# Moving the attention keys next to their batch, fixing the places of the first feed-forward, and moving one product behind the last transposes

## The chip, the core and the metric

The kernel runs on one core of a Trainium2 chip. Its engines work side by side and each takes its own instructions in order: PE (TensorE, matrix products and transposes, with a weight load PEld ahead of each), DVE (VectorE), ACT (ScalarE), POOL (GpSimd) and SP, which here only issues transfers. The metric is the device time of one execution in microseconds (us).

## The reference

Four batches of 512 tokens with 512 features pass through four residual steps. `ctx` holds 512 tokens of 128 features for each batch.

```python
x = x + tanh(g_xattn[0]) * L0_xattn(ctx, layernorm(x))   # learned adjacency
x = x + tanh(g_ffn[0])   * L0_ffn(layernorm(x))          # Hadamard, 8-bit, ternary weights
x = x + tanh(g_xattn[1]) * L1_xattn(layernorm(x), ctx)   # 16 heads, latent keys
x = x + tanh(g_ffn[1])   * L1_ffn(layernorm(x))          # rms norm, 8-bit, ternary weights

# L0_xattn: sim = Q K^T of ctx; in each row the 153 largest are kept (threshold), sigmoid,
#           A = (A + A^T) / 2, and a mix with the normalised x
# L0_ffn:   h = fwht(x) quantised to 8 bits; u = silu(h Wg) * (h Wu); fwht(u) quantised; u Wd
# L1_xattn: q_big = rope(x Wq w_kc_q), kv_r = rope(ctx)
#           q_r = q_big W_qr, k_r = kv_r W_kr          (64 numbers for each of the 16 heads)
#           attn = softmax(q_r k_r^T); ctx_c = attn kv_r; out = ctx_c w_kc_kv Wo
# L1_ffn:   value * silu(gate) of quantised x, quantised, w_out
```

The keys `k_r` depend on `ctx` alone, and those of a batch are first needed when that batch's attention begins.

## The kernel before

The kernel has three stages: a prologue for batch 0, the attention of all four batches with the other work woven between its steps, and a tail with the last feed-forward of batch 3. The flag `alone[0]` is true in the prologue and in the tail.

**Prologue.** Three generators are stepped by turns: `adjacency(0)` (the top-k of batch 0, 20 rounds of `max` and `match_replace` for each tile of 128 rows, lines 436 and 441), `feed_weights` (ternary weights for the first feed-forward) and `ahead()`. `ahead()` rotates `ctx` into `kv` for all batches on POOL, multiplies the two output matrices of each of the 16 heads into one (`pO`, line 668, copied by ACT and stored to DRAM as `omd`), transposes the four `kv` (`pkv`, line 678), and then makes the keys: for each of 8 pairs of heads one weight `wk` is loaded (line 685), and for each of the four batches one product `pk` of 128x512 (line 688), one ACT copy to `krs` (line 690), and one store by POOL's queue to the DRAM tile `krd` (line 692). Attention loads `kr` back from `krd` (line 783). The feed-forward of batch 0, `feed0(0)`, follows; `ahead()` is stepped once for each of its steps.

**The first feed-forward.** Each of four tiles is normalised, turned and quantised; its gates (`pg`, `pu`, line 291) are multiplied into `ya` (line 297); `back` runs four butterfly stages of two halves each between `ya` and `yb` on DVE (line 538), four transposes and small Hadamard products on PE (`ph`, line 544, and `pzh`, line 550) with ACT copies between, the largest value `amaxh` (line 364; in four parts at line 359 for the last tile), the quantisation to `q` (lines 369 and 197), transposes of `q` (`ptq_h`, line 191) and the down product `pd` (line 386). `big()` gives `ya` and `yb` their place: while `alone`, three of five calls take the ring `big` of three buffers, and two take the ring `pT` of two, by a counter that the weight loads use too. A ring's next tile waits for the readers of the tile that had its buffer.

**Attention.** It walks through 32 pairs of heads, 8 for each batch. In each of four steps `j` of a pair it computes scores (`pss`, lines 806 and 809), their largest value (`nm`, line 814, DVE), the exponentials (line 817, ACT) and the division (line 820); it transposes the probabilities two steps later (`turn`, `ppt`, line 828, copied to `pT` at line 829). Between these stand the queries of the next pair: `head` (`pqh`, line 747) and `rope` (`pb`, line 762, then `ro` and `rs` on DVE, lines 770 to 775, and their sum on POOL, line 776). At the end of a pair `rotated()` loads `kr` and multiplies the rotated queries into `q_r` (`pr`, lines 733 and 735; ACT copy `qr`, line 793), the last two `turn` follow, then `attended` (`pc`, line 836) and `added` (`po`, line 848, with the sum on DVE at line 853).

**What is woven in.** `jobs` holds for each batch `b` from 1 to 3 a generator `before(b)`: `adjacency(b)`, then `feed0(b)`; it must be finished when the attention of batch `b-1` ends. The last job makes the ternary weights of the second feed-forward and runs `feed1` of batches 0 to 2. After each step of a pair the loop takes as many steps of the job as its costs allow.

**What sets the order.** The source order is a priority only: a scheduler places each instruction on its engine. `tc.high_priority(offset=-FILL)` with `FILL = 800` gives the top-k a lower priority, so that it fills DVE between the attention's own instructions. PSUM has the pools `mm` (4 banks), `tr` (2) and `bg` (2). `bg_tr` gives every fourth transpose a `bg` bank while `alone`, otherwise every one. `front_t` alternates between the rings `front` (3 buffers) and `pp` while `alone`, otherwise it takes `front`.

Of the kernel before, what the change touches and what calls it, by code (L numbers as in the profile page):

```python
# [9 lines left out]
F32 = mybir.dt.float32  # L10
BF = mybir.dt.bfloat16
# [4 lines left out]
P = 128  # L16
B, S, D = 4, 512, 512
NT = S // P
NC = D // P
FF = 2048  # L20
# [13 lines left out]
def flamingo_kernel(  # L34
# [9 lines left out]
    nc = tc.nc  # L44
# [4 lines left out]
    dram = ctx.enter_context(tc.tile_pool(name="dram", bufs=1, space=bass.MemoryType.DRAM))  # L49

    bp = ctx.enter_context(tc.tile_pool(name="bg", bufs=1))
    hp = ctx.enter_context(tc.tile_pool(name="heads", bufs=2))
    wp = ctx.enter_context(tc.tile_pool(name="attn", bufs=2))
# [4 lines left out]
    def mm_ps(name):  # L58
        return ps.tile([P, 512], F32, tag="mm", name=name)

    def tr_ps(name):
        return pst.tile([P, 4, P], F32, tag="tr", name=name)


    alone = [True]
# [9 lines left out]
    def gate_ps(name):  # L75
        return mm_ps(name) if alone[0] else bg_ps(name)

    def bg_tr(name, dt=F32):
        if mine("tr", 4):
            return psb.tile([P, 4, P], dt, tag="bg", name=name)  # L80
        return pst.tile([P, 4, P], dt, tag="tr", name=name)

    def two_k(tag, bufs, name):
        return bp.tile([P, 512], F32, tag=tag, name=name, bufs=bufs)

    def front_t(name):
        if mine("front", 2):
            return two_k("front", 3, name)
        return wp.tile([P, 512], F32, tag="pp", name=name, bufs=7)
# [6 lines left out]
    def back_t(name):  # L96
        return two_k("back", 2, name)

    def big(name):
        turn_of["big"] += 1  # L100
        if not alone[0] or turn_of["big"] % 5 in (1, 3, 0):
            return bp.tile([P, FF], F32, tag="big", name=name, bufs=3)
        t = wp.tile([P, NT, S], F32, tag="pT", name=name)
        return t.rearrange("p j s -> p (j s)")

    ident = const.tile([P, P], F32, tag="ident", name="ident")
# [32 lines left out]
    def drain(gen):  # L139
        try:  # L140
            while True:
                next(gen)
        except StopIteration as e:
            return e.value
# [157 lines left out]
    def tiles(name, ready, wa, back, spread):  # L302

        def gate(j):
            zq, dg, du = ready[j]
            y = big(f"ya_{name}_{j}")
            return gated(f"{name}_{j}", zq, wa, dg, y), back(j, y, du)  # L310

        def go(gen, parts):
            for _ in range(parts):
                next(gen, None)

        if not alone[0]:
            last = iter(())
            for j in range(NT):
                if j == 2:
                    reached.append(name)  # L320
                front, behind = gate(j)
                yield from woven(front, last)
                last = behind
            yield from last
            return
        front, cur = gate(0)
        drain(front)
        last = None
        for j in range(NT):
            front, after = gate(j + 1) if j + 1 < NT else (iter(()), None)  # L330
            for k in range(8 if spread else 4):
                if spread:
                    go(cur, 1)
                if k % 2 == 0 or not spread:
                    go(front, 1)
                yield 0.0
            if spread:
                if last:
                    go(last, 4)
                go(cur, 4)  # L340
            else:
                go(cur, 4)
            if last:
                drain(last)
            last, cur = cur, after
        drain(last)
        yield 0.0
# [47 lines left out]
    FILL = 800  # L395
# [240 lines left out]
    NG = NH // 2  # L636
# [4 lines left out]
    def ahead():  # L641

        cos_k = wp.tile([P, NT, DC], F32, tag="rs", name="cos_k", bufs=3)
        nc.gpsimd.dma_start(cos_k, cosk)
        sin_k = wp.tile([P, NT, DC], F32, tag="rs", name="sin_k", bufs=3)
        nc.gpsimd.dma_start(sin_k, sink)
        kvT = []
        hf = DC // 2  # L650
        for b in range(B):
            cb = wp.tile([P, NT, DC], F32, tag="qh", name=f"cb_{b}")
            nc.gpsimd.dma_start(cb, cx[b * S : (b + 1) * S, :].rearrange("(j p) d -> p j d", p=P))
            t = const.tile([P, NT, DC], F32, tag=f"kv{b}", name=f"kv_{b}")
            nc.gpsimd.tensor_tensor(t, cb, cos_k, ALU.mult)
            rt = wp.tile([P, NT, DC], F32, tag="rs", name=f"rt_{b}", bufs=3)
            nc.gpsimd.tensor_tensor(rt[:, :, :hf], cb[:, :, hf:], sin_k[:, :, :hf], ALU.mult)
            nc.gpsimd.tensor_tensor(rt[:, :, hf:], cb[:, :, :hf], sin_k[:, :, hf:], ALU.mult)
            nc.gpsimd.tensor_tensor(t, t, rt, ALU.add)
            kv[b] = t  # L660
        yield
        for h in range(NH):
            wv = hp.tile([P, DC], F32, tag="wk", name=f"wv_{h}", bufs=3)
            nc.sync.dma_start(wv, wkckv[h])
            wo = wp.tile([P, D], F32, tag="rs", name=f"wo_{h}", bufs=3)
            nc.sync.dma_start(wo, woT[h])
            po = mm_ps(f"pO_{h}")
            nc.tensor.matmul(po, wv, wo, start=True, stop=True)
            om = wp.tile([P, D], F32, tag="cxo", name=f"oms_{h}", bufs=3)
            nc.scalar.copy(om, po)  # L670
            d = dram.tile([P, D], F32, tag=f"om{h}", name=f"omd_{h}")
            nc.gpsimd.dma_start(d, om)
            om_d[h] = d
            yield
        for b in range(B):
            pt = tr_ps(f"pkv_{b}")
            for j in range(NT):
                nc.tensor.transpose(pt[:, j, :], kv[b][:, j, :], ident)
            tT = two_k("gate", 2, f"kvT_{b}") if b < 2 else hp.tile([P, S], F32, tag="om", name=f"kvT_{b}")
            nc.scalar.copy(tT, pt.rearrange("p j q -> p (j q)"))  # L680
            kvT.append(tT)
            yield
        for g in range(NG):
            wk = hp.tile([P, P], F32, tag="wk", name=f"wk_{g}", bufs=3)
            nc.sync.dma_start(wk, wkr[g])
            for b in range(B):
                pk = mm_ps(f"pk_{b}_{g}")
                nc.tensor.matmul(pk, wk, kvT[b], start=True, stop=True)
                k = wp.tile([P, S], F32, tag="cxo", name=f"krs_{b}_{g}", bufs=3)
                nc.scalar.copy(k, pk)  # L690
                d = dram.tile([P, S], F32, tag=f"kr{b}_{g}", name=f"krd_{b}_{g}")
                nc.gpsimd.dma_start(d, k)
                kr_d[b, g] = d
                yield

    def hidden_T(b):
        mv, r = ln_stats([xs[b, j] for j in range(NT)], f"q{b}")
# [162 lines left out]
    def attention(first):  # L860


        order = [(b, g) for b in range(B) for g in range(NG)]
        cur = first
        for at, (b, g) in enumerate(order):
            nxt = begin(*order[at + 1]) if at + 1 < len(order) else None
            cur.oms = out_weights(b, g)
            fresh = nxt is not None and nxt.b != b
            for j in range(NT):
                cur.scores(j)  # L870
                if nxt:
                    if j == 0:
                        if fresh:
                            hidden_T(nxt.b)
                        nxt.head(0)
                    elif j == 1:
                        nxt.rope(0)
                        nxt.head(1)
                    elif j == 2:
                        nxt.rope(1)  # L880
                    else:
                        nxt.rope(2)
                if j > 1:
                    cur.turn(j - 2)
                yield b, g
            if nxt:
                nxt.rotated()
            cur.turn(NT - 2)
            cur.turn(NT - 1)
            cur.attended()  # L890
            cur.added()
            if g == NG - 1 and b < B - 1:
                for j in range(NT):
                    d = dram.tile([P, D], F32, tag=f"xd{b}_{j}", name=f"xd_{b}_{j}")
                    nc.sync.dma_start(d, xs[b, j])
                    spilled[b, j] = d
            cur = nxt
# [5 lines left out]
    def step(gen, parts):  # L903
        for _ in range(parts):
            next(gen, None)
# [38 lines left out]
    w1 = []  # L944

    def before(b):
        yield from adjacency(b)
        yield from feed0(b, w0)

    def last_weights():  # L950
# [164 lines left out]
```

## Time and profile before

| | us |
|---|---|
| median of 3 runs | 2082.72 (2080.54 to 2085.15) |
| the profiled execution | 2086.76 |
| its span, first to last instruction | 2085.0 |
| first scores of the attention (copy of the first `qr`) | 290.0 |
| `qr` copies of the first pairs of batches 1, 2, 3 | 701.9, 1123.1, 1544.4 |
| `qr` copy of the last pair | 1923.4 |

The profile lists busy times of the engines; a row of a group ends with the idle time before it and with what ended it. A matmul with 32-bit operands stands in the records as two halves. In timelines the first two numbers are start and duration, and square brackets give the idle time of the engine before the instruction and what it waited for.

### The profile page before, as it was taken

Reading aid. Unit: us, or ns where it says so; the run is one execution under the profiler, and the core shown is the slowest. Engines: PE = TensorE matmul, PEld = TensorE weight load, DVE = VectorE, ACT = ScalarE, POOL = GpSimd, SP = SyncE. Lnnn points to the kernel's source line nnn. Section 1 sums busy time; section 2 is a strip of 40 time slices with the busy share of each in tenths; the row PEclk is TensorE's granted clock in tenths of the full one; section 3 lists DMA queues with packets and bytes.
Section 4 is the critical chain, followed back from the end, with each engine's and each line's share of the span. In section 5 each row is a group of like instructions: output and inputs, shape, how many; then the busy total and the mean of one; then the engine's idle time right before and its main releaser. Section 6 shows DMA issues by size and latency. Waiting matters only on the chain.

```text
span 2085.0 us, 21677 instructions
## 1 busy us (share of the span) xinstructions
PE 1864.1 (89%) x7274; PEld 876.8 (42%) x7274; DVE 1589.9 (76%) x3233; ACT 1182.9 (57%) x1982; POOL 331.0 (16%) x316
## 2 busy tenths in 40 slices
PE   1269889999999999999989999999889999999898
PEld 0135433444544444444544444445443444444444
DVE  6997689996675999967668999676645745856775
ACT  6936634354744554455455553554799565567554
POOL 3011121122101121131011211310111200111000
PEclk9779989999999999999999999999999999999999
DMA  7442211110100211111002111110656111111000
GB/s 268 149 141 107 83 37 48 44 46 27 38 20 27 86 50 41 47 32 33 25 27 87 49 47 38 37 33 20 224 185 225 55 31 46 57 32 46 11 16 26
DMA packets 62175, 137.66 MB, mean 66 GB/s; under 512 B 7152, under 2 KB 14704, under 8 KB 58992
## 3 DMA queue, kind: packets, MB, share of 16 engines
q1 hardware_dynamic: 56592, 120.35, 18.2%
q0 software_dynamic: 4320, 14.16, 1.8%
q10 hardware_dynamic: 1152, 1.77, 0.2%
q8 instruction: 58, 0.95, 0.2%
q14 instruction: 53, 0.43, 0.1%
HBM read 116.33 MB, written 19.92 MB: 65 GB/s over the span
## 4 chain that ended last, share of the span: by engine, by line
PE 52%; DVE 29%; ACT 11%; DMA 3%; POOL 2%; issue 2%; ACTq 0%; SPq 0%; POOLq 0%; DVEq 0%
PE pc L836 8%; PE po L848 6%; PE pqh L747 6%; DVE work L441 4%; DVE m L436 4%; DVE nm L814 4%; PE pb L762 3%; PE pzh_f L550 3%; PE pr L733 3%; PE pss L806 3%; PE pu_f L291 2%; DVE rs L775 2%; PE pg_f L291 2%; DVE ro L770 2%; PE pu_g L291 2%; PE pd_g L386 2%
## 5 line engine op out<-in xcount | busy, mean ns | idle before, releaser
L776 POOL TENSOR_TENSOR ro<-ro,rs 128x512 f32<-128x512 f32 x192 | 250.3, 1306 | 1333.8 <-DVE rs L772 722.5
L817 ACT ACTIVATE pp<-pss,nm 128x512 f32<-128x512 f32 x256 | 175.1, 688 | 224.6 <-DVE nm L814 223.9
L747 PE MATMUL pqh<-hT,wq 128*128 128x512 f32 x512 | 240.6, 609 | 4.0 <-ACT pp L817 2.5
L836 PE MATMUL pc<-pT,kv 128*128 128x512 f32 x512 | 233.5, 598 | 6.0 <-ACT pT L829 6.0
L848 PE MATMUL po<-om,cxo 128*128 128x512 f32 x512 | 231.4, 596 | 0.5 <-ACT cxo L841 0.5
L814 DVE TENSOR_REDUCE nm<-pss 128x1 f32<-128x512 f32 x256 | 167.6, 680 | 70.4 <-PE pss L809 70.0
L762 PE MATMUL pb<-qh,wc 128*128 128x512 f32 x384 | 191.7, 617 | 7.4 <-DVE ro L770 3.8
L436 DVE MAX8 m<-work 128x8 f32<-128x512 f32 x304 | 197.6, 680 | 0.5
L441 DVE MATCH_REPLACE8 work<-m,work 128x512 f32<-128x512 f32 x288 | 192.9, 675 | 0.1
L820 ACT ACTIVATE pp<-pp,rsm 128x512 f32<-128x512 f32 x256 | 179.2, 725 | 17.7 <-DVE rsm L819 17.1
L829 ACT COPY pT<-ppt 128x512 f32<-128x512 f32 x256 | 143.2, 590 | 36.9 <-PE ppt L828 36.8
L828 PE MATMUL ppt<-ident,pp 128*128 128x128 f32 x1024 | 149.3, 280 | 11.4 <-ACT pT L829 9.2
L853 DVE SCALAR_TENSOR_TENSOR x<-po,gt,x 128x512 f32<-128x512 f32 x128 | 94.5, 743 | 82.6 <-PE po L848 81.5
L828 PEld LDWEIGHTS ppt<-ident,pp 128*128 128x128 f32 x1024 | 116.4, 142 | 92.5 <-issue 45.6
L806 PE MATMUL pss<-kr,qr 64*128 64x512 f32 x256 | 145.6, 649 | 9.0 <-ACT pp L817 7.5
L747 PEld LDWEIGHTS pqh<-hT,wq 128*128 128x128 f32 x512 | 93.7, 193 | 126.9 <-issue 93.1
L809 PE MATMUL pss<-kr,qr 64*128 64x512 f32 x256 | 145.5, 649 | 0.0
L848 PEld LDWEIGHTS po<-om,cxo 128*128 128x128 f32 x512 | 94.4, 190 | 113.7 <-issue 95.7
L770 DVE TENSOR_TENSOR ro<-pb,cos_q 128x512 f32<-128x512 f32 x192 | 130.4, 679 | 15.1 <-PE pb L762 14.3
L836 PEld LDWEIGHTS pc<-pT,kv 128*128 128x128 f32 x512 | 93.0, 191 | 102.8 <-issue 90.5
L733 PE MATMUL pr<-ro,wr 128*64 128x512 f32 x192 | 100.6, 625 | 29.5 <-POOL ro L776 28.3
L841 ACT COPY cxo<-pc 128x512 f32<-128x512 f32 x64 | 37.5, 586 | 135.3 <-PE pc L836 135.1
(266 smaller groups left out, 3132.8 us busy)
## 6 DMA issues: line engine op xcount, KB each, us to landing
wq<-in_wqh SPq DMA_DIRECT2D x64, 256.0 KB, 2.7
om<-omd SPq DMA_DIRECT2D x64, 256.0 KB, 2.7
wc<-in_wkcq SPq DMA_DIRECT2D x32, 384.0 KB, 3.1
krd<-krs POOLq DMA_DIRECT2D x32, 256.0 KB, 2.5
kr<-krd SPq DMA_DIRECT2D x32, 256.0 KB, 2.7
sa_w1v<-in_gvT SPq DMA_DIRECT2D x8, 1024.0 KB, 5.6
sb_w1v<-in_gvT SPq DMA_DIRECT2D x8, 1024.0 KB, 5.5
wr<-in_wqr SPq DMA_DIRECT2D x32, 192.0 KB, 2.4
```

The lines of the kernel that those rows point to most:

```text
L436: nc.vector.max(m8[j], cur[j])
L441: nc.vector.match_replace(works[j], m8[j], cur[j], GONE)
L747: nc.tensor.matmul(pq, self.wqs[i][:, c, :], hT[self.b][:, c, :], start=(c == 0), stop=(c == NC - 1),)
L762: nc.tensor.matmul(pb, self.wc[:, at : at + P], self.qhs[i if i < 2 else o], start=True, stop=True)
L776: nc.gpsimd.tensor_tensor(ro, ro, rs, ALU.add)
L806: nc.tensor.matmul(*args, start=True, stop=True)
L814: nc.vector.tensor_reduce(nm, pss[i], AX.X, ALU.max, negate=True)
L817: nc.scalar.activation(pp, pss[i], AF.Exp, bias=nm, accum_out=sm)
L820: nc.scalar.activation(pp, pp, AF.Copy, scale=rs)
L828: nc.tensor.transpose(pt[:, l, :], pp[:, l * P : (l + 1) * P], ident)
L836: nc.tensor.matmul(pc, kv[self.b][:, l, :], self.pT[i][:, l, :], start=(l == 0), stop=(l == NT - 1),)
L848: nc.tensor.matmul(po, self.cxo[i][:, j * P : (j + 1) * P], self.oms[i], start=(i == 0), stop=(i == 1),)
```

## The change

1. Of the keys, `ahead()` makes only those of batch 0. A new generator `keys(b)` makes those of one batch: it transposes `kv[b]`, copies it to a tile in the ring `q`, and for each pair of heads loads `wk`, multiplies, copies and stores. `before(b)` steps it once for every sixth step of `adjacency(b)`, at a priority lower by 200. Each batch loads the 8 weights anew: 32 loads where there were 8.
2. In the feed-forward of batch 0 the eight calls of `big()` take their places from a list: `b` is the ring `big`, `t` the ring `pT`, and `h` the buffer `hT`, which the adjacency of batch 0 had and which the transposed input of the attention takes next. In the order of the calls they are ya 0, ya 1, yb 0, ya 2, yb 1, ya 3, yb 2, yb 3.
3. `nxt.rotated()` stands behind the last two `turn`.

```diff
+    lent = []
+
     def big(name):
+        place = lent.pop(0) if lent else None
+        if place == "h":
+            t = hp.tile([P, NC, S], F32, tag="hT", name=name, bufs=1)
+            return t.rearrange("p c s -> p (c s)")
+        if place == "t":
+            t = wp.tile([P, NT, S], F32, tag="pT", name=name)
+            return t.rearrange("p j s -> p (j s)")
+        if place == "b":
+            return bp.tile([P, FF], F32, tag="big", name=name, bufs=3)
         turn_of["big"] += 1
...
+        if spread:
+            lent.extend("btbhtbbt")
         front, cur = gate(0)
         drain(front)
...
-        for b in range(B):
-            pt = tr_ps(f"pkv_{b}")
-            for j in range(NT):
-                nc.tensor.transpose(pt[:, j, :], kv[b][:, j, :], ident)
-            tT = two_k("gate", 2, f"kvT_{b}") if b < 2 else hp.tile([P, S], F32, tag="om", name=f"kvT_{b}")
-            nc.scalar.copy(tT, pt.rearrange("p j q -> p (j q)"))
-            kvT.append(tT)
+        yield from keys(0)
+
+    def keys(b):
+
+        pt = bg_tr(f"pkv_{b}")
+        for j in range(NT):
+            nc.tensor.transpose(pt[:, j, :], kv[b][:, j, :], ident)
+
+        kvT = bp.tile([P, FF], BF, tag="q", name=f"kvT_{b}").bitcast(F32)[:, 0:S]
+        nc.scalar.copy(kvT, pt.rearrange("p j q -> p (j q)"))
+        yield
+        for g in range(NG):
+            wk = hp.tile([P, P], F32, tag="wk", name=f"wk_{b}_{g}", bufs=3)
+            nc.sync.dma_start(wk, wkr[g])
+            pk = gate_ps(f"pk_{b}_{g}")
+            nc.tensor.matmul(pk, wk, kvT, start=True, stop=True)
+            if alone[0]:
+                k = wp.tile([P, S], F32, tag="cxo", name=f"krs_{b}_{g}", bufs=3)
+            else:
+                k = front_t(f"krs_{b}_{g}")
+            nc.scalar.copy(k, pk)
+            d = dram.tile([P, S], F32, tag=f"kr{b}_{g}", name=f"krd_{b}_{g}")
+            nc.gpsimd.dma_start(d, k)
+            kr_d[b, g] = d
             yield
-        for g in range(NG):
-            wk = hp.tile([P, P], F32, tag="wk", name=f"wk_{g}", bufs=3)
-            nc.sync.dma_start(wk, wkr[g])
-            for b in range(B):
-                pk = mm_ps(f"pk_{b}_{g}")
-                nc.tensor.matmul(pk, wk, kvT[b], start=True, stop=True)
-                k = wp.tile([P, S], F32, tag="cxo", name=f"krs_{b}_{g}", bufs=3)
-                nc.scalar.copy(k, pk)
-                d = dram.tile([P, S], F32, tag=f"kr{b}_{g}", name=f"krd_{b}_{g}")
-                nc.gpsimd.dma_start(d, k)
-                kr_d[b, g] = d
-                yield
...
+            cur.turn(NT - 2)
+            cur.turn(NT - 1)
             if nxt:
                 nxt.rotated()
-            cur.turn(NT - 2)
-            cur.turn(NT - 1)
...
     def before(b):
-        yield from adjacency(b)
+        k = keys(b)
+        for n, cost in enumerate(adjacency(b)):
+            yield cost
+            if n % 6 == 5:
+
+                with tc.high_priority(offset=-FILL // 4):
+                    step(k, 1)
+        drain(k)
         yield from feed0(b, w0)
```

## The prediction

> **What bounds the kernel now.** I read the page first, then busy time by windows, the pk tile, the DVE timeline of the prologue, and the PE waits of the attention.
>
> The page says that PE is the busiest engine, and that its bad slices are the first six (the prologue, before the first scores at 290 us) and the tail:
>
> ```profile
> PE 1864.1 (89%) x7274; PEld 876.8 (42%) x7274; DVE 1589.9 (76%) x3233; ACT 1182.9 (57%) x1982; POOL 331.0 (16%) x316
> ...
> PE   1269889999999999999989999999889999999898
> ...
> DVE  6997689996675999967668999676645745856775
> ...
> PEclk9779989999999999999999999999999999999999
> ```
>
> By windows (us; then PE, PEld, DVE, ACT, POOL busy, granted clock, DMA share, GB/s) the feed-forward of batch 0 has a middle where PE never rests, and edges where it does:
>
> ```profile
> 125.00:150.00 25.00, 13.75 (x69) 8.80 (x68) 19.98 (x61) 8.87 (x16) 1.62 (x3) 0.73 0.16 56
> 150.00:175.00 25.00, 24.84 (x116) 13.10 (x115) 24.86 (x51) 15.37 (x25) 4.31 (x8) 1.00 0.31 111
> 175.00:200.00 25.00, 24.95 (x147) 15.54 (x145) 14.78 (x18) 19.40 (x33) 5.34 (x9) 1.00 0.27 101
> 200.00:225.00 25.00, 24.82 (x119) 13.48 (x119) 24.84 (x32) 15.87 (x28) 6.59 (x12) 1.00 0.33 124
> 225.00:250.00 25.00, 19.43 (x128) 12.45 (x126) 14.53 (x29) 14.00 (x24) 1.62 (x3) 1.00 0.18 58
> ```
>
> The key products lie in exactly this middle:
>
> ```profile
> L688 PE MATMUL pk<-kvT,wk x64: 592/592/648, 156.7 to 231.9; 128*128 128x512 f32 x64
> L690 ACT COPY krs<-pk x32: 566/586/657, 158.1 to 232.5; 128x512 f32<-128x512 f32 x32
> ```
>
> The 64 records are 32 products; a group of four records fills 1.72 us of the chain, so one costs PE 0.86 us, 27.5 us for all. The DVE timeline shows who is late for it: the gate of tile 3 waits 6.44 us for PE, then the butterfly of tile 2 2.33 us:
>
> ```profile
> 183.17 2.28 DVE L364 TENSOR_REDUCE amaxh_f<-yb_f 128x1 f32<-128x2048 f32 x1
> ...
> 196.47 0.69 DVE L297 TENSOR_TENSOR ya_f<-sg_f,pu_f 128x512 f32<-128x512 f32 x1 [6.44 <-PE pu_f L291]
> 199.49 2.36 DVE L538 TENSOR_TENSOR yb_f<-ya_f 128x1024 f32<-128x1024 f32 x2 [2.33 <-PE ph_f L544]
> ...
> 228.85 2.29 DVE L364 TENSOR_REDUCE amaxh_f<-yb_f 128x1 f32<-128x2048 f32 x1 [1.12 <-ACT yb_f L551]
> ```
>
> In the attention, the first four pairs of a batch carry the top-k of the next batch's adjacency. There both PE and DVE are nearly full, DVE more so; the last four carry the feed-forward and are PE's:
>
> ```profile
> 701.90:742.80 40.90, 38.92 (x121) 16.49 (x122) 40.51 (x95) 20.82 (x40) 7.62 (x6) 1.00 0.31 98
> 742.80:782.90 40.10, 38.51 (x118) 16.30 (x119) 39.91 (x92) 17.54 (x37) 7.64 (x6) 1.00 0.16 48
> 782.90:824.10 41.20, 38.64 (x125) 16.80 (x125) 39.27 (x86) 22.36 (x43) 7.61 (x6) 1.00 0.17 47
> 824.10:864.80 40.70, 38.52 (x122) 16.39 (x122) 40.22 (x92) 17.78 (x37) 7.62 (x6) 1.00 0.17 47
> 864.80:1123.10 258.30, 245.97 (x1035) 122.71 (x1036) 184.20 (x328) 133.38 (x245) 43.53 (x40) 0.98 0.11 32
> ```
>
> What PE waits for from 290 us on (total, times, longest): above all the last rotated chunk of the next pair, added on POOL, in front of q_r's product:
>
> ```profile
> PE pr L733 <- POOL ro L776: 24.1, 23, 1.6
> PE ppt L828 <- ACT pT L829: 9.2, 29, 1.6
> ...
> PE pc L836 <- ACT pT L829: 6.0, 16, 1.9
> ```
>
> **Part 1, keys moved: the prologue.** By the built order, 13 products stay ahead of the first scores (8 of batch 0, 5 of batch 1), so PE loses 19 x 0.86 = 16.3 us there, and 8 transposes of 0.13 = 1.0; ACT loses 19 copies of 0.58. Were PE the only bound, that would be 17 us of gain. It is not, because DVE and the chain of one tile are late next. DVE needs, from tile 0's first butterfly (155.9) to tile 3's last (226.8), 70.9 us, of which it waited 0.5+0.9+6.4+2.3 = 10.1. That is all it can give, and not all comes:
> - Three batch-0 products now stand on PE between the last pO and adjacency's transposes padj (started 127.42, first sum at 129.32). The third needs a weight slot that the last pO frees at 127.6 and a load of 2.1 us (wk's median landing), so padj starts near 131: DVE is 2.5 us later from there on.
> - The new order puts the gates of tiles 2 and 3 first, and the amaxh of tile 0 behind ya of tile 2 and the whole butterfly of tile 1. Adding DVE's starts in that order (butterfly half 1.14, gate 0.60, amaxa 0.61, h 0.7), and 2.5 us for the last pu of tile 2, which stands behind tile 0's Hadamards on PE, amaxh of tile 0 falls at 189, tile 0's turned q at 198 (before 191.0).
> - Behind that one tile costs: turned q to yb complete 235.30 to 245.75 = 10.45, about 9.1 in the new order, which pairs the transposes (1.3 us of PE-ACT ping-pong less); amaxh to the next turned q 6.6 (2.28, 0.9, 1.29, 2.0). Tile 1 is held by DVE (217, before 217.9), tile 2 comes at 233 (235.3), the last at 245.0 (248.7). So -3.7.
>
> Fixed places: ya of tile 2 goes to hT, yb of tile 2 to tile 0's place, yb of tile 3 to the place of tile 1, free early. What they remove is the 2.33 us wait above, already in the 10.1; hT is free again before hidden_T (264 us). At the end of the prologue batch 1's first products fill the place of two psim and two table loads; the fifth, ahead of the last pb, may cost 0.9: 0 to +1.
>
> The clock speaks against this part. Row: in 125:150 the granted clock was 0.73 after a PE pause of 5.98 us, while 175:225, kept full by pk, had 1.00. [...] Without pk, PE pauses some 5 to 7 us between a tile's pd and the next turned q, twice. By the rows of 225:250 (pause 2.8, clock 1.00) nothing is lost; [...] I take +0.7, as PE is only part of that chain. Prologue: -3.0, ends -9 (no padj delay, no gate wait) and +2.
>
> **Part 2, keys moved: the attention.** PE takes on the 16.3 + 1.0 there, and two psim (1.7): 19 us. Three products fall into batch 0's pairs, eight in each of batches 1 and 2. Twenty-four loads of wk (64 KB) join SP's queue, in front of wc and wr of the next pair; those have a pair of lead (40 us), hidden; uncovered, 2.1 us each. On POOL, 24 stores of 0.54 us stand among the rotation adds; POOL is busy 7.6 of 40 us, and the store waits for a copy that ACT makes right behind pk, so I put 0; where one is late, the add behind it and q_r wait, up to 1 us in a pair. ACT's added copies: 3 x 0.58 in a pair with 18 to 22 of 40 us busy: 0.
>
> **Part 3, q_r behind the last transposes.** The source moves all of it; the built order moves less. Before the last two pr, PE has in the first pairs of batch 0 only 0.1 to 0.3 us more work than before, in the fourth even less, but in batches 1 and 2 1.3 to 4.4 us more (keys included). Of the 24.1 us I count 13 recovered. qr has 14 us of pc and po between it and the next scores, so nothing else waits for it. Transposes of four tiles in a row over two buffers can cost 0.2 to 0.5 a pair (the ppt row); the pc row gives about as much back.
>
> **The sum by batches**, PE and DVE work counted by the built order with the trace's starts:
> - Batch 0, pairs 0-3: DVE 163.7 before, 163.8 after, so 0. Pairs 4-7: PE -1.4, POOL waits 3.4, of which 2: -3.5 (ends -8, +2).
> - Batch 1, pairs 0-3 (162.9 us): PE +10.3 (6.9 of keys, the rest feed-forward pulled ahead), DVE +3.7, since the top-k is packed forward: pairs 0-3 get 1.3, 4.4, 2.5 more, then 4.5 less. If PE ran through but for half its waits, +6; if each pair takes its larger engine, 42.6+44.3+43.6+42.5 = 173, +10. I take +8. Pairs 4-7 (258.3 us): PE -2.9 and half of the waits there: -6. So +2 (ends -2, +8). Batch 2 has the same order: +2.
> - Batch 3 and the last pair of 2: POOL waits of 3.3 us, most gone: -2.7 (ends -5, +2). The tail after 1923 has the same order: 0.
>
> Together -3.0 -3.5 +4 -2.7 = -5.2. The profiled execution took 2086.8 (span 2085.0, 1.8 around it), the median is 2082.7, 4.0 lower; the difference is applied to the median: 2077.5.
>
> **Rivals.**
> - *Slower: DVE becomes the bound of the adjacency pairs.* Packed top-k gives pairs 0-2 of batches 1 and 2 DVE work of 42.2, 43.9, 43.2 against PE's 40.2, 42.5, 41.3, then PE bounds pair 3. It decides once a pair's DVE work passes PE's by the waits that q_r gave back, about 1 us. Then +10 in four pairs, only -2.9 behind: +14 for both batches; with -3 elsewhere 2093, with the other parts as above 2089. For it: DVE's idle time there is 0.2 to 0.5 us a pair. Against: before, such pairs carried 40.9 of DVE in 40.9. Centre 2090.
> - *A wash: 19 us of PE work moved into full pairs, against 13 of waits and the prologue.* 2083, within 4. For it: PE's total work is the same before and after.
> - *The prologue is PE's after all*: padj is not late and the tiles' chains overlap; -12 there and the attention as above: 2068. For it: PE at 24.9 of 25 us; against: the 14.5 us of DVE in 225:250, a chain with no engine full.
> - *q_r does not move*: that is the wash, by the built order.
>
> **Numbers.** About 0.2% (4.2 us) can be told from no change. Forecast 2077.5, own range 2070 to 2081: 0.38; prologue rival 0.12; wash 0.25; slower 0.25. So faster 0.50, same 0.25, slower 0.25. Signs are mixed, so the range reaches to both: 2065 to 2092.
>
> **What would show it.** First scores near 287; amaxh of tile 0 near 189 and padj near 131; PE waits for POOL ro of about 11 us after 290; pairs 0-3 of batch 1 at 171 us together, DVE idle under 0.6 in three of them. Wrong if the prologue ends before 281 (chain misread), if those four pairs stay below 166 (PE and DVE overlap better), or if pr still waits 20 us.

## The result

The changed kernel takes 2064.13 us (median of 6 runs, 2061.82 to 2073.35) against 2083.93 us for the kernel before, measured beside it: ratio 0.9907, 95% interval 0.9883 to 0.9931. Run once more beside the experiments it took 2067.17 us, ratio 0.9918 (0.9903 to 0.9932). The gain is 17 to 20 us where 5 were forecast.

The profiled execution took 2064.35 us, span 2062.6. The page of the changed kernel, busy totals and rows of 40 slices:

```profile
PE 1853.7 (90%) x7274; PEld 873.3 (42%) x7274; DVE 1584.7 (77%) x3233; ACT 1176.6 (57%) x1979; POOL 333.1 (16%) x316
...
PE   1268789999999999999999999999999999999898
...
PEclk6579899999999999999999999999999999999999
```

PE's busy time fell by 10.4 us though the work is the same (the 7274 records are as many as before). The prologue of the changed kernel by windows (us; then PE, PEld, DVE, ACT, POOL busy, granted clock, DMA share, GB/s), and the first turned `q` of each tile on PE:

```profile
150.00:175.00 25.00, 24.82 (x120) 12.24 (x119) 24.82 (x57) 15.54 (x24) 2.69 (x5) 1.00 0.23 77
175.00:200.00 25.00, 20.07 (x123) 12.80 (x122) 24.38 (x32) 14.21 (x22) 0.00 (x0) 0.88 0.00 1
200.00:225.00 25.00, 17.57 (x117) 14.34 (x116) 20.38 (x29) 11.60 (x19) 0.00 (x0) 0.84 0.00 1
225.00:250.00 25.00, 19.80 (x126) 13.72 (x126) 12.48 (x25) 14.21 (x23) 0.00 (x0) 0.86 0.00 1
```
```profile
196.72 1.89 PE L202 MATMUL ptq_hf<-identb,q_f 128*128 128x128 bf16 x16 [3.99 <-ACT q_f L208]
...
216.21 1.89 PE L202 MATMUL ptq_hf<-identb,q_f 128*128 128x128 bf16 x16 [6.84 <-ACT q_f L208]
...
233.00 1.89 PE L202 MATMUL ptq_hf<-identb,q_f 128*128 128x128 bf16 x16 [3.67 <-ACT q_f L208]
...
246.35 0.40 PE L202 MATMUL ptq_hf<-identb,q_f 128*128 128x128 bf16 x4
```

PE now has holes where the keys were, and the granted clock falls to 0.84 to 0.88 behind them. Yet the first `qr` copy comes at 284.5 in place of 290.0. The pairs of batch 1 by windows, one by one and the last four together:

```profile
689.40:730.40 41.00, 39.67 (x125) 17.16 (x125) 40.12 (x96) 21.41 (x42) 8.20 (x7) 1.00 0.31 100
730.40:776.10 45.70, 43.47 (x133) 18.42 (x134) 45.06 (x101) 23.39 (x46) 9.79 (x10) 1.00 0.25 76
776.10:817.30 41.20, 39.62 (x122) 16.98 (x123) 40.98 (x92) 21.89 (x43) 9.23 (x9) 1.00 0.24 70
817.30:859.00 41.70, 39.35 (x129) 17.21 (x129) 41.13 (x91) 19.65 (x41) 7.61 (x6) 1.00 0.17 47
859.00:1106.10 247.10, 239.46 (x1033) 119.21 (x1033) 174.56 (x309) 129.14 (x241) 44.96 (x40) 1.00 0.11 33
```

The first four pairs are 6.6 us longer than before (169.5 against 162.9 between the `qr` copies) and the last four 11.1 us shorter (247.2 against 258.3). In their row the granted clock went from 0.98 to 1.00, and 0.02 of 258 us is 5 us. What PE waits for from 284.5 on (total, times, longest):

```profile
PE pr L750 <- POOL ro L793: 10.2, 11, 1.4
...
PE ppt L845 <- ACT pT L846: 3.5, 9, 0.7
...
PE pc L853 <- ACT pT L846: 0.6, 3, 0.2
...
PE ptq_hf L202 <- DVE q_f L210: 0.6, 2, 0.3
```

The wait of `pr` fell from 24.1 to 10.2 as forecast. Three other waits fell too, and of these the last is new here: before, the transposes of `q` (`ptq_h`) waited 8.0 us for DVE's `q_f` in the attention, 3.4 at once, and the prediction did not list it:

```profile
PE ptq_hf L191 <- DVE q_f L199: 8.0, 4, 3.4
```

Some waits rose: that of `pb` for ACT's `qh` from 3.1 to 7.3 us, that of `pqh` for ACT's `pp` from 2.5 to 6.6.

By sections, in us between `qr` copies of the profiled executions, with the length of the stretches in which the trace's clock record of PE stands at one half:

| section | before | forecast change | changed kernel | again | half clock before | after |
|---|---|---|---|---|---|---|
| to the first `qr` | 290.0 | -3.0 | 284.5 | 283.1 | | |
| batch 0, pairs 0-3 | 151.5 | 0 | 149.6 | 149.6 | 5.8 | 0 |
| batch 0, pairs 4-7 | 260.3 | -3.5 | 255.3 | 255.3 | 13.7 | 10.2 |
| batch 1, pairs 0-3 | 162.9 | +8 | 169.5 | 169.7 | 0 | 0 |
| batch 1, pairs 4-7 | 258.3 | -6 | 247.2 | 247.2 | 10.2 | 0 |
| batch 2, pairs 0-3 | 162.9 | +8 | 169.7 | 169.4 | 0 | 0 |
| batch 2, pairs 4-7 | 258.4 | -6 | 250.1 | 249.6 | 10.2 | 6.8 |
| batch 3 to the last `qr` | 379.0 | -2.7 | 376.9 | 377.7 | 3.4 | 0 |
| tail | 161.5 | 0 | 159.8 | 162.2 | | |

From the first scores to the end it is 1794.9 us before and 1778.1 and 1780.6 after: -14 to -17 where the sum said -2.2. A part of this belongs to the one execution of the kernel before that was profiled. Part 2 alone (below) leaves the order of PE's and ACT's instructions in the attention as it was, and its profiled execution took 1789.7 us there, 5.2 less, with 42.0 us of half clock in attention and tail in place of 57.6. Against the mean of the two, 1792.3, the three executions of the changed order (1778.1, 1780.6, and 1780.5 without part 2) gain 12.6.

### The profile page after: what moved, and what is told of

It is laid out like the page before. It is cut to its first block, busy times and chain, and to the rows that moved or that the text cites. A ratio compares the mean times of both kernels' runs of the same rounds, so it can differ in the third digit from the quotient of the medians.

```text
span 2062.6 us, 21752 instructions
## 1 busy us (share of the span) xinstructions
PE 1853.7 (90%) x7274; PEld 873.3 (42%) x7274; DVE 1584.7 (77%) x3233; ACT 1176.6 (57%) x1979; POOL 333.1 (16%) x316
## 5 line engine op out<-in xcount | busy, mean ns | idle before, releaser
L779 PE MATMUL pb<-qh,wc 128*128 128x512 f32 x384 | 191.1, 614 | 10.4 <-ACT qh L769 7.3
L787 DVE TENSOR_TENSOR ro<-pb,cos_q 128x512 f32<-128x512 f32 x192 | 130.5, 680 | 11.0 <-PE pb L779 10.2
L750 PE MATMUL pr<-ro,wr 128*64 128x512 f32 x192 | 99.8, 613 | 14.3 <-POOL ro L793 12.2
```

Source lines behind the costliest of these rows:

```text
L779: nc.tensor.matmul(pb, self.wc[:, at : at + P], self.qhs[i if i < 2 else o], start=True, stop=True)
```

## The experiments

All ratios are to the kernel before, measured beside the run. "Attention" is the stretch from the first `qr` copy to the end of the profiled execution.

**Each part alone, and each left out.** Part 3 alone, on the kernel before:

```diff
-            if nxt:
-                nxt.rotated()
             cur.turn(NT - 2)
             cur.turn(NT - 1)
+            if nxt:
+                nxt.rotated()
```

> The kernel before with part 3 alone: q_r's line behind the last two transposes. Theory A (q_r carries the unforeseen gain: each removed wait of pr for POOL's last rotated chunk is a PE pause of up to 1.6 us, and such pauses also halved the clock, as at 490.4 and 913.6 in the trace of before): pr's waits for POOL after the prologue fall from 24.1 us to under 12, the half-speed stretches at 490 and 914 go, and the time falls by about 15 us, to 2069. Theory B (the keys carry it: fuller PE in the prologue's end and another order of the feed-forward in pairs 4 to 7 of batches 1 and 2): about -5, to 2079, with the 3.4 us waits for q_f in pairs 6 of batches 1 and 2 and their half-speed stretches still there. My forecast's own terms (half of the waits) would give about -6.

Measured: 2069.98 us, ratio 0.9947 (0.9935 to 0.9959), attention 1781.3 (-13.6). Waits of PE after the prologue in this kernel:

```profile
PE pr L733 <- POOL ro L776: 14.4, 18, 1.8
PE ptq_hf L191 <- DVE q_f L199: 8.0, 4, 3.4
...
PE ppt L828 <- ACT pT L829: 7.7, 21, 0.7
...
PE pc L836 <- ACT pT L829: 0.2, 1, 0.2
```

Nearer to theory A in time, but by another way than it says. `pr` gains 9.7 us, not over 12, and `pc` gains 5.8 more: q_r's product now stands between the last transposes and `pc`, where ACT makes its last copies of `pT`. The stretches at 490 and 914 went as theory A says, but others came: attention and tail have 57.6 us of half clock, as before. The one edit shortened two waits.

The changed kernel with part 3 undone (the same edit backwards):

> The changed kernel with part 3 undone: q_r's line again ahead of the last two transposes, keys and fixed places as in the changed kernel. Theory A (q_r carries the unforeseen gain): the time is about 2079, 5 under before, pr waits 20 us or more for POOL, and the clock is halved in pairs 4 again. Theory B (keys carry it): about 2069, 15 under before, and the pairs 4 to 7 of batches 1 and 2 are still some 8 us shorter each than before.

Measured: 2086.93 us, ratio 1.0020 (1.0011 to 1.0029), attention 1798.3; slower than before, and worse than either theory. `pr` waits 22.2 us and `pc` 5.1. Pairs 4 to 7 of batches 1 and 2 are 251.3 and 251.5 us, so 7 shorter than before, as theory B had it, but pairs 0 to 3 are 172.2 and 172.7, so 9 to 10 longer.

Part 1 alone (the keys' generator in `before(b)`, places and q_r as before):

> The kernel before with part 1 alone: the keys of batches 1 to 3 beside their own adjacency, places and q_r as before. Theory A (q_r carries it): prologue 5 us shorter, pairs 0 to 3 of batches 1 and 2 some 7 us longer each, pairs 4 to 7 some 3 shorter: about 2083, no change. Theory B (keys carry it): pairs 4 to 7 of batches 1 and 2 some 10 us shorter each, half-speed stretches in the attention down from 37.5 us to under 20: about 2069. If the fixed places are needed to let the prologue gain, the first scores are within 2 us of 290.

Measured: 2089.94 us, ratio 1.0036 (1.0023 to 1.0048), attention 1798.1. The keys alone cost 5 to 10 us, theory B falls. Its second half holds in direction: half clock between the first and the last `qr` is 20.5 us in place of 43.3 (the 37.5 of the expectation leaves out the first pairs of batch 0), and pairs 4 to 7 of batches 1 and 2 are 7 us shorter. The first scores came at 289.6.

Part 1 undone, so parts 2 and 3:

> The changed kernel with part 1 undone, that is the kernel before with parts 2 and 3: all keys in the prologue again, fixed places and q_r as changed. Theory A: about 2069 (q_r alone gives it, the keys nothing). Theory B: about 2078. The first scores stay within 2 us of 290 if the prologue's gain is the keys', and come 2 to 3 us earlier if the places alone gave it.

Measured: 2066.59 us, ratio 0.9926 (0.9910 to 0.9942), attention 1779.6, first scores at 285.2. Theory A: nearly the whole gain is there without the keys' move. The first scores came 4.8 us early, which points at the places.

Part 2 undone, and part 2 alone:

```diff
-        if spread:
-            lent.extend("btbhtbbt")
```

> The changed kernel with part 2 undone: parts 1 and 3 alone, places of batch 0's feed-forward by turn as before. Theory A (the places are worth some 3 to 4 us whatever stands beside them, as the pairs of runs with and without them show so far): first scores 3 us or more later than in the changed kernel, ratio to before 0.992 to 0.993. Theory B (they matter only for the clock's luck in the prologue): no difference from the changed kernel, 0.9907 within 0.001. The attention from the first scores on takes 1778 us within 2 by both.

> The kernel before with part 2 alone: fixed places for the first feed-forward of batch 0. Theory A (the places are worth 3 to 4 us by themselves): ratio to before 0.998 to 0.9985, the attention from the first scores on as before, 1795 us within 2. Theory B (they only matter together with the keys' move, which puts other transposes into their way): ratio 1.000 within 0.001.

Measured: without the places 2067.52 us, ratio 0.9923 (0.9910 to 0.9936); the places alone 2080.05 us, ratio 0.9983 (0.9975 to 0.9991). Alone they are worth 2 to 5 us. Beside the other parts they can't be told from nothing, since the changed kernel gave 0.9907 and 0.9918. The attention took 1780.5 us without the places, near the 1778 expected, and 1789.7 with the places alone, 5 below what both theories said.

The three alone give 0.9947 x 1.0036 x 0.9983 = 0.9966, or -7 us; together they give -17 to -20. The parts that need each other are the keys and q_r: q_r's move is worth 11 us without the keys (0.9947) and 23 beside them (from 1.0036 to 0.9923); in the attention alone 13.6 against 17.6 (from 1798.1 to 1780.5 us). With the places in both it is the same: 12 us (0.9983 to 0.9926) and 21 to 24 (1.0020 to 0.9918 and 0.9907).

The traces say where the difference does not lie. The next table splits the attention by PE: its idle time; half of its busy time in stretches at half clock, an estimate of what the slow clock cost; and the rest of its busy time, here called work. All are us. Each row is one order of PE's instructions in the attention, with the executions that have it.

| order | attention | idle | slow clock | work |
|---|---|---|---|---|
| before; places alone | 1794.9, 1789.7 | 105.0, 106.6 | 24.8, 17.3 | 1665.1, 1665.8 |
| q_r moved; with places | 1781.3, 1779.6 | 88.2, 90.1 | 26.3, 22.3 | 1666.8, 1667.2 |
| keys moved; with places | 1798.1, 1798.3 | 99.1, 100.0 | 16.0, 15.7 | 1683.0, 1682.6 |
| both; both with places, twice | 1780.5, 1778.1, 1780.6 | 85.0, 86.8, 86.7 | 16.1, 12.4, 14.3 | 1679.4, 1678.9, 1679.7 |

q_r's move saves 17 us of idle time without the keys and 13 beside them, so its greater worth beside them is not one of waits: it stands in the work (+1.6 and -3.5 us) and in the slow clock (+3.2 and -1.6). The keys' move adds 17 us of work, or 12 beside q_r's move, and there the smaller loss to the slow clock (10 us) and to idle time (3 us) pays for it.

**The changed kernel again.**

> The changed kernel once more, unchanged, beside the others: how far one execution's prologue and attention repeat. If the executions differ in the prologue alone, the stretch from the first scores to the end is 1778.1 us within 1, and the first scores fall between 280 and 289; if the attention's clock varies by chance from run to run, that stretch differs by some 3 to 10 us. Ratio to before 0.9907, as measured.

Measured: ratio 0.9918, first scores at 283.1, attention 1780.6 against 1778.1. That is more than 1 and less than 3, so between the two cases. The pairs repeat within 0.8 us by section; the rest is the tail, 2.4. The first scores are at 281.8 to 289.6 in the eight profiled executions with the keys moved (mean 284.9) and at 285.2 to 291.2 in the six without (mean 288.0), so single executions of the prologue differ by more than the keys' move does.

**The pauses and the clock.** A first trial was to fill the two 3.37 us pauses of the kernel without part 1 with useless work:

```diff
             pt = bg_tr(f"ptq_{name}_{k}", BF)
+            if name in ("hf2_2", "hf3_2") and k == 0:
+                for c in range(26):
+                    nc.tensor.transpose(pt[:, c % 4, :], identb, identb)
```

> The kernel of the run without part 1 (parts 2 and 3 alone), with 26 more transposes of the identity (0.12 us each at full clock, 3 us) into the bank of ptq_hf ahead of the first turned h of tile 2, in batches 2 and 3 only; real transposes then overwrite them, so the result is the same. They are useless work that fits in the two pauses of 3.37 us in which PE waits for q_f and after which the clock was halved for 6.8 us, at 1030 and at 1450. Theory A (a pause costs its half-speed stretch on top of itself, and what the keys bring in the attention is that they fill pauses): both stretches go, the same feed-forward work takes 3.4 us less twice, and the time falls by 6 to 7 us against that run, ratio to before 0.989 to 0.990, although 6 us of PE work were added. Theory B (the clock's records don't matter, only the work does): no change or up to 6 us slower, ratio 0.9926 to 0.9955.

Measured: 2065.72 us, ratio 0.9912 (0.9893 to 0.9931), attention 1780.7. It settles nothing. The 26 transposes took 1.6 us, or 0.06 us each, not 3 (0.12 us each is what such transposes took at half clock: in the changed kernel 16 took 1.89 us at 196.72, within the stretch from 194.2 to 201.0), and they did not stand in the pause:

```profile
1026.18 1.61 PE L203 MATMUL ptq_hf<-identb 128*128 128x128 bf16 x26
...
1036.67 0.67 PE L205 MATMUL ptq_hf<-identb,q_f 128*128 128x128 bf16 x8 [1.87 <-DVE q_f L213]
```

They ran 7 us ahead of it and pushed PE's other work back, into the wait. Pauses of 1.87 and 1.86 us were left, and behind each the clock was halved all the same, for 6.8 and 3.4 us.

The second takes away what PE waits for. In the kernel without part 1, DVE did this ahead of the `q_f` that PE waited for until 1030.65:

```profile
1021.00 2.29 DVE L377 TENSOR_REDUCE amaxh_f<-yb_f 128x1 f32<-128x2048 f32 x1 [0.15 <-ACT yb_f L564]
1023.20 1.21 DVE L551 TENSOR_TENSOR ya_f<-yb_f 128x1024 f32<-128x1024 f32 x1
...
1024.46 1.22 DVE L551 TENSOR_TENSOR ya_f<-yb_f 128x1024 f32<-128x1024 f32 x1
...
1025.91 1.21 DVE L551 TENSOR_TENSOR yb_f<-ya_f 128x1024 f32<-128x1024 f32 x1
1027.05 1.28 DVE L382 TENSOR_SCALAR yb_f<-yb_f,s_hf 128x2048 f32<-128x2048 f32 x1
1028.24 1.22 DVE L551 TENSOR_TENSOR yb_f<-ya_f 128x1024 f32<-128x1024 f32 x1
1029.38 1.22 DVE L210 TENSOR_SCALAR q_f<-yb_f 128x2048 bf16<-128x2048 f32 x1
```

Four butterfly halves of the next tile (L551) stand inside the chain of this one. The edit lowers their priority, in `back` of the first feed-forward:

```diff
-                    nc.vector.tensor_tensor(*args)
+                    with tc.high_priority(offset=-40) if j == NT - 1 and not alone[0] else ExitStack():
+                        nc.vector.tensor_tensor(*args)
```

On the kernel without part 1:

> Parts 2 and 3 without the keys' move, and one thing more: the butterfly of the last tile of a feed-forward beside attention gets a lower priority by 40, so that on DVE it no longer stands between tile 2's amax and its rounded q_f; in the runs without the keys' move four such halves (1.2 us each) stood there and PE waited 3.37 us for q_f in pairs 6 of batches 1 and 2, after which its clock was halved for 6.8 us. Theory A (what the keys' move brought in pairs 4 to 7 was this pause and its half-speed stretch, by a chance of DVE's order): the waits for q_f fall from 8.0 to about 3 us, the stretches at 1030 and 1450 go, pairs 4 to 7 of batches 1 and 2 fall from 255.3 and 260.2 to about 249 and 253 us, and the time falls by 8 to 13 us against the run without keys: ratio to before 0.986 to 0.989, faster than the changed kernel. Theory B (the keys shorten these pairs because feed-forward work goes ahead into pairs 0 to 3, and the pause is hidden or taken over by another wait): ratio 0.9926 within 0.0015.

Measured: 2060.54 us, ratio 0.9885 (0.9867 to 0.9904), 6 to 9 us better than without it, the waits for `q_f` down from 8.0 to 3.8. Pairs 4 to 7 are 250.3, 251.7 and 255.4 us in batches 0, 1, 2, against 255.3, 255.3 and 260.2. Both stretches went; in batch 2 one of 10.2 us came up in their place, in a new wait of 6.7 us of `phT` for the normalised `x`, and batch 3 took 383.6 us in place of 377.1, with a new wait of 5.0 us of `pc`. So the edit changed more than the pause. That is 3.6 and 4.8 of the 8.1 and 10.1 us that the keys' move brings to these pairs of batches 1 and 2, so theory A explains at most that. The rest, some 5 us a batch, fits theory B, that work goes ahead into pairs 0 to 3; it was not tried by itself.

On the changed kernel:

> The changed kernel with the same lower priority for the last tile's butterfly. Theory A (the changed kernel has lost this pause already, 0.6 us of waits for q_f are left): no change, ratio to before 0.990 to 0.992, pairs 4 to 7 of batches 1 and 2 within 1 us of 247.2 and 250.1; with the run beside it the keys' move then costs some 4 to 8 us where this pause is gone without it. Theory B (the keys shorten these pairs by themselves): this kernel stays about 3 us ahead of the run beside it.

Measured: 2058.80 us, ratio 0.9869 (0.9849 to 0.9889). This is the fastest kernel of the study, 8 to 10 us ahead of the changed one by the two ratios of that. Batches 1 and 2 are as expected (247.1 and 250.1); the gain is in batch 0, which the expectation had forgotten: its pairs 4 to 7 fall from 255.3 to 248.6. Theory B is not borne out: this kernel is 1.7 us ahead of the run beside it, and the intervals overlap, so where the pause is gone the keys' move can't be told from nothing. The gain in batch 0 is one pair. The changed kernel around its pause, then that pair as a window, then the same pair of the faster kernel:

```profile
614.03 2.07 PE L823 MATMUL pss<-kr,qr 64*128 64x512 f32 x2 [2.50 <-ACT pp L834]
616.04 1.03 PE L202 MATMUL ptq_hf<-identb,q_f 128*128 128x128 bf16 x8
```
```profile
564.10:637.10 73.00, 70.26 (x305) 36.03 (x306) 49.56 (x69) 35.36 (x67) 8.50 (x6) 0.93 0.09 27
```
```profile
562.60:628.60 66.00, 65.09 (x297) 33.23 (x298) 49.28 (x69) 34.18 (x64) 10.51 (x6) 1.00 0.10 30
```

The pause of 2.50 us is gone, idle time falls from 2.74 to 0.91, PE's busy time from 70.26 to 65.09, the clock rises from 0.93 to 1.00. In the changed kernel the clock was at one half for 10.2 us from 614.0 on, and half of that is 5.1: the 7.0 us between the two are 1.8 of waiting and 5.2 of slow work (8 of 305 records have gone to a neighbouring pair; the section as a whole is 6.7 us shorter). In the changed kernel three butterfly halves stood on DVE between `amaxh` (605.25) and `nm` (612.49), for whose exponentials PE waited; in the faster kernel `nm` follows `amaxh` at once, at 605.98.

**Where the keys stand.** The fastest kernel with the keys beside the feed-forward, in place of the adjacency:

```diff
     def before(b):
+        yield from adjacency(b)
         k = keys(b)
-        for n, cost in enumerate(adjacency(b)):
+        for n, cost in enumerate(feed0(b, w0)):
             yield cost
-            if n % 6 == 5:
+            if n % 2 == 1:
                 with tc.high_priority(offset=-FILL // 4):
                     step(k, 1)
         drain(k)
-        yield from feed0(b, w0)
```

> The changed kernel with the lower priority for the last tile's butterfly, and the keys of batches 1 to 3 behind the adjacency, beside the first feed-forward in pairs 4 and 5, in place of beside the adjacency in pairs 0 to 3. Theory A (in pairs 0 to 3 DVE bounds, at 45.1 of 45.7 us in the longest, and the keys lengthened these pairs by pulling top-k and feed-forward work forward, while in pairs 4 to 7, where DVE rests 15 to 20 us in each pair, only PE's 0.9 us a product count): pairs 0 to 3 of batches 1 and 2 fall from 169.6 to about 162 us, pairs 4 to 7 rise from 247.1 and 250.1 by 5 to 7, so 1 to 4 us faster in all, ratio 0.985 to 0.9865. Theory B (PE bounds both, and a product costs the same wherever it stands; the pairs are only cut elsewhere): pairs 0 to 3 fall by 8, pairs 4 to 7 rise by 8 to 10, ratio 0.987 to 0.989.

Measured: 2077.32 us, ratio 0.9971 (0.9960 to 0.9982). Theory A is wrong and theory B too mild. Batches 1 and 2 of this kernel by windows, pairs 0 to 3 and 4 to 7:

```profile
695.70:858.00 162.30, 155.94 (x485) 66.17 (x485) 159.72 (x360) 79.32 (x157) 30.50 (x24) 1.00 0.20 60
858.00:1115.40 257.40, 248.33 (x1053) 122.61 (x1054) 183.43 (x328) 140.35 (x255) 49.02 (x48) 1.00 0.14 42
1115.40:1277.00 161.60, 155.97 (x485) 66.21 (x486) 159.67 (x361) 79.34 (x158) 30.50 (x24) 1.00 0.21 62
1277.00:1539.00 262.00, 248.28 (x1042) 124.67 (x1042) 175.07 (x309) 161.06 (x268) 49.03 (x48) 0.97 0.29 95
```

Pairs 0 to 3 fall by 7.3 and 8.0 us, and the others rise by 10.3 and 11.9, with 8.6 and 10.5 us more of busy PE. Batch 0, which now makes all of batch 1's keys, has pairs 4 to 7 of 259.7 us in place of 248.6. (The edit also makes the keys in quicker steps, one for every second step in place of every sixth; this was not tried apart.) The idle DVE there buys nothing, and the place beside the adjacency is the better one, though it makes those pairs DVE's.

**q_r one step further back.** `attended` takes the head's number, and the order becomes:

```diff
             cur.turn(NT - 1)
+            cur.attended(0)
             if nxt:
                 nxt.rotated()
-            cur.attended()
+            cur.attended(1)
             cur.added()
```

> The changed kernel with q_r's line one step further back: behind the first head's pc and ahead of the second's. Theory A (what is left to gain is in the 10.2 us in which pr still waits for POOL's last rotated chunk): pr's waits fall under 3 us, and the time falls by 7 to 10 us against the changed kernel, ratio to before 0.986 to 0.987. Theory B (q_r's product was also the cover for ACT's last copies of pT ahead of pc, 6.0 us of waits before and 0.6 in the changed kernel; without it they come back): pc's waits for ACT are 4 us or more again and the time stays within 3 us of the changed kernel, ratio 0.990 to 0.992.

Measured: 2105.35 us, ratio 1.0107 (1.0090 to 1.0125). Both theories are wrong: A had the waits of `pr` right and the time wrong, B looked for the cost at `pc`. No wait of `pr` for POOL is left in the list, and `pc` waits 1.3 us, but the transposes wait:

```profile
PE ppt L845 <- ACT pT L846: 23.1, 40, 2.8
...
PE ppt L845 <- ACT pp L837: 9.9, 4, 2.9
```

Pairs 0 to 3 of batches 1 and 2 take 187 us, 17 to 18 more, with 13.7 us of half clock in each batch where the changed kernel has none. Why the scheduler's order becomes so much worse was not taken apart.

## Why the prediction was wrong

- *Prologue, -3.0.* The times were right, the cause mostly not, and the pair of traces shown gains 5.5. `padj` came at 130.85 (forecast near 131), `amaxh` of tile 0 at 187.78 (189), turned `q` at 196.7, 216.2, 233.0 and 246.4 (198, 217, 233, 245). But the first turned `q` of the last tile, at 248.7 and 249.9 in the two executions with neither the keys' move nor the places, came at 245.9 to 247.5 in the four with the places and without the keys' move, and at 251.5 and 247.3 in the two the other way round. So the forecast put the places at nothing beyond a wait already counted, and they brought most of what it gave to the keys; that these times fit is luck in part. The other 3.2 us lie behind the last `pd`: from there to the first `qr` it is 35.2 to 35.6 us in the five executions with a stretch of half clock that begins between 262 and 267 us, that of the kernel before among them, and 31.9 to 32.8 in the nine without one. Of four executions with the places and without the keys' move, all with one order on PE up to there, two have that stretch, so it comes by chance; of the five with the changed kernel's order there, none has it.
- *The clock there, +0.7.* That was the author's estimate, from a row of before with a pause of 2.8 us and the clock at 1.00. The clock fell further than it allowed for: the changed kernel's pauses of 3.99, 6.84 and 3.67 us ahead of the turned `q` stand with three stretches of 6.8 us at half speed, from 194.2, 214.7 and 231.8 on. Charging little for them did no harm: the turned `q` came within 2 us of the forecast all the same.
- *`pr`: 13 of 24.1 us recovered.* Right: 13.9. But the forecast set the gain of `pc` against a loss of `ppt`. `pc` gave 5.4 us, and `ppt` gave 5.7 instead of losing.
- *Pairs 0 to 3 of batches 1 and 2, +8 each.* Near: +6.5 to +6.8. The slower rival's mechanism is real: DVE is idle 0.2 to 0.9 us in each of these pairs (under 0.6 in two of batch 1, where the forecast said three).
- *Pairs 4 to 7, -3.5, -6 and -6.* This is where the sum failed most: -5.0, -11.1 and -8.3, so 8.9 us of the error. The sum took PE work by order and half of `pr`'s waits. It left out the pause for `q_f`, and the clock altogether: the stretches at half speed in these pairs fell from 34.1 to 17.0 us, which is worth 8.5 by the pair of traces shown, and 6 if the two executions of the order before (34.1 and 23.8) and the three of the order after (17.0, 13.6 and 20.5) are averaged. The clock was weighed in the prologue, where the change makes pauses, and not in the attention, where there were pauses to lose. Both were in the views: `q_f` in the list of waits, 0.98 in the row of pairs 4 to 7.
- *The step that failed, over the whole attention.* In the forecast's terms its -2.2 us is +13.4 of PE work (-1.4, and twice 10.3 less 2.9), -15.6 of waits, and nothing for the clock. By the means of the table above the work rose by 13.9 us, PE's idle time fell by 19.6 and the loss to the slow clock by 6.8, which is the gain of 12.6 but for rounding. So the work was right. The larger miss is the clock, put at nothing without a reason; the smaller is the waits of `pc`, `ppt` and `q_f` beside `pr`'s.
- *The rivals.* Moved PE work did not make a wash: the keys' work shows in the attention, and yet beside q_r's move they cost nothing there (1778.1 and 1780.6 against 1779.6 without them), since the slow clock took less. Without q_r's move they cost 3 to 8 us (1798.1 against 1794.9 and 1789.7). "q_r does not move" fell; it is the part that carries the gain.
- *Small slips, which move nothing.* The four terms behind `amaxh` add to 6.5, not 6.6; the slower rival with the other parts as above is 2087.5, not 2089; and DVE's idle time of 0.2 to 0.5 us in such a pair leaves out the third row shown, with 1.9.

What stays open: why q_r's move saves work and slow clock beside the keys and not alone. It isn't the waits.

## What to carry to other kernels

Where a product waits for another engine and a neighbour waits for a copy, one move can cover both (part 3 alone took 9.7 us from the waits of `pr` and 5.8 from those of `pc`); look at what stands on either side of the new place, and what could be put there, before pricing the edit by its own wait alone. Price a pause of TensorE as its length plus half of the slow stretch that may follow: without its pause of 2.50 us the pair at 614 was 7.0 us shorter, 1.8 of waiting and 5.2 of slow work. A granted clock of 0.98 over 258 us is 5 us that an edit can win or lose by chance of order, and that one execution can win or lose with the order unchanged (the loss to the slow clock was 24.8 and 17.3 us in two executions of one order): profile a kernel more than once before the clock is called a cause. Work moved into a full stage should be priced by the whole stage, not by the pairs that it lands in: beside q_r's move the keys cost their pairs 8 us a batch, and the next four pairs gave back 8 to 10.

## What the runs showed of the hardware

All 25 pauses of PE of 2.4 us or more in the attention of the fourteen profiled executions (first to last `qr` copy) had a stretch at half speed beginning in them or within 1.2 us of their end; so had 20 of the 91 pauses from 1.4 to 2.4 us, and none of the 287 from 0.75 to 1.4. In the traces of the kernel before and of the changed kernel these are 4 of 4, 4 of 12 and none of 46. The clock record tells more of the difference. It reads full or one half. In each execution every change between full and half clock, 418 apart from the end of the record, lies within 4 ns on a grid of 3.413 us (58 of them in the two traces named, within 3 ns). Cut the attention along this grid, and take the 6533 pieces at full clock. Where PE's records fill less than 0.45 of a piece, the next piece ran at half clock in 32 of 33 cases; from 0.45 to 0.55 in 25 of 46; above that in none of 6454. In the two traces named it is 4 of 5, 5 of 7 and none of 919.

In the kernel before, a wait of 1.55 us for POOL's `ro` at 911.9 fell into one piece (from 910.20 to 913.61, filled to 0.47), and the next ran at half clock. A wait of 1.54 us at 1333.1, for the same thing, was cut by an edge at 1333.45 (0.82 and 0.66), and the clock stayed full. The product behind the first took 0.97 us, that behind the second 0.64:

```profile
913.42 0.97 PE L733 MATMUL pr<-ro,wr 128*64 128x512 f32 x1 [1.55 <-POOL ro L776]
```

The grid lies differently against the program in each execution (its first edge behind the first `qr` copy comes 0.6 to 2.4 us after it). That fits what the table of the attention shows, the same order of work losing 24.8 us to the slow clock in one execution and 17.3 in another. Behind pieces that were idle for about half of it the clock was often halved (25 of 46). So, as an estimate from these counts, taking half a microsecond off a 1.5 us wait can be worth 1.7 us more than that (half of a piece of 3.413 us), or nothing more.
